# Sixteen half-width products in place of four full ones, in one aggregation of a stack of graph layers in fp32

## The chip, the cores and the metric

The kernel runs on one core of one Trainium2 chip. The metric is the device time of one execution in microseconds (us). In this text TensorE (PE in the profile) does the matmuls, ScalarE (ACT) the activations, VectorE (DVE) the elementwise work.

## The reference, cut to what matters

32 graphs of 512 nodes with 128 features pass four layers, each with its own normalisation and residual. The change touches one line of the last layer, the product of the adjacency matrix with the messages:

```
def _L3_gnn_ref(h, A, W_msg, b_msg, W_ih, b_ih, W_hh, b_hh):
    ...
    msg_pre = jnp.einsum('bnh,kh->bnk', h, W_msg) + b_msg
    m = jnp.tanh(jnp.einsum('bnm,bmh->bnh', A, msg_pre))      # <- this product
    gi = jnp.einsum('bnh,kh->bnk', m, W_ih) + b_ih
    ...
```

## The kernel before

The kernel does not issue its instructions where they are written. Each is recorded with an engine, a duration, what it reads and what it writes. A planner, a small simulation with a priority queue for each engine, then interleaves the 32 graphs and issues everything in the order that this simulation found. The framework below it still moves some instructions.

```
def t_mm(n):
    return n * 0.00167 + 0.008            # us planned for a matmul of n columns

# ... cut ...
def mm(ps, out_of, lhs, rhs, n, start, stop, reads, part=None):
    op("PE", t_mm(n), lambda: nc.tensor.matmul(out_of(ps.ap()), lhs(), rhs(), start=start, stop=stop),
       reads, [(ps, part) if part is not None else ps])

# ... cut ...
def aggregate(ps, feats, lo, m, start=True, stop=True):
    for c in range(NC):                   # NC = 4 blocks of 128 nodes
        mm(ps, lambda t: t, lambda c=c: feats.ap()[:, c, lo:lo + D], lambda c=c: m.ap()[:, c, :], N,
           start and c == 0, stop and c == NC - 1, [(feats, {c}), (m, {c})])
# ... layers 0 to 2 left out ...
psa = plan.bank("agg")
aT2 = buf("s8", (P, NC, N), "aT2")
# ... aT2 is loaded ...
aggregate(psa, msg, 0, aT2)               # D = 128 output rows, N = 512 columns, 4 matmuls
mT = buf("s2", name="mT")
op("ACT", t_act(N), lambda: nc.scalar.activation(mT.ap(), psa.ap(), AF.Tanh), [psa], [mT])
```

Elsewhere each normalisation ends on ScalarE, which writes a tile `h` in four pieces, and TensorE then transposes each piece into `ps_t`.

Of the kernel before, what the change touches and what calls it, by code (L numbers as in the profile page):

```python
# [19 lines left out]
B, N, D = 32, 512, 128  # L20
NC = N // P
# [186 lines left out]
def gnn_stack(  # L208
# [33 lines left out]
    def t_mm(n):  # L242
        return n * 0.00167 + 0.008
# [10 lines left out]
    def op(*args, **kwargs):  # L254
        return plan.op(*args, **kwargs)
# [10 lines left out]
# [3 lines that stand above are left out]
# [58 lines left out]
    def program(b):  # L327
        plan.batch = b

        def buf(tag, shape=(P, N), name=None):  # L330
            return plan.buf(tag, shape, name)
# [57 lines left out]
        def aggregate(ps, feats, lo, m, start=True, stop=True):  # L389

            for c in range(NC):
                mm(ps, lambda t: t, lambda c=c: feats.ap()[:, c, lo:lo + D], lambda c=c: m.ap()[:, c, :], N,
                   start and c == 0, stop and c == NC - 1, [(feats, {c}), (m, {c})])
# [163 lines left out]
        msg = buf("s2", rows_shape, "msg")  # L557
        tt(msg, lambda: nc.vector.tensor_add(msg.ap(), psm.ap().rearrange("p (c v) -> p c v", c=NC), along(r_sb, R_L3_MSG, D, NC)),  # L558
           N, [psm, RS])
        psa = plan.bank("agg")  # L560
        aT2 = buf("s8", (P, NC, N), "aT2")
        op("SP", 0.1, lambda: nc.sync.dma_start(aT2.ap(), adjt[b].rearrange("(c p) n -> p c n", p=P)), [], [aT2], land=5.3)
        aggregate(psa, msg, 0, aT2)
        mT = buf("s2", name="mT")
        op("ACT", t_act(N), lambda: nc.scalar.activation(mT.ap(), psa.ap(), AF.Tanh), [psa], [mT])

# [27 lines left out]
    for b in range(B):  # L594
        program(b)
# [41 lines left out]
```

## Time and profile before

| | before |
|---|---|
| time | 2489.16 us median of 2 runs (2486.97 to 2491.35) |
| TensorE busy | 2419.9 of 2485.6 us |
| next engine, VectorE, busy | 1136.9 us |
| the product that changes | 128 matmuls, 256 records |

The prediction below shows how this is read. Columns: who waited for whom, total us, number of waits, longest us.

```profile
PE ps_agg L267 <- DVE sd L418: 9.9, 22, 0.6
PE ps_t L383 <- ACT h L375: 8.8, 3, 4.1
```

TensorE hardly ever stands still for another engine: 8.8 us for the transposes of `h`, in three waits.

### The profile page before, as it was taken

The page shows a single profiled execution, that of the slowest core. Times are in us where ns is not written, and L with a number is a line of the kernel's source. Part 1 is how long each engine was busy: PE and PEld are TensorE (multiplying, and loading weights), DVE is VectorE, ACT ScalarE, POOL GpSimd, SP SyncE. Part 2 cuts the span into 40 slices and gives each one's busy share as a digit, 9 for nine tenths or more (in the row PEclk, how much of TensorE's full clock was granted, in tenths as well). Part 3 has the DMA queues.
Part 4 walks back from the last instruction along what each step waited for, and adds up shares of the span by engine and source line. Part 5 has one row for each costly group of instructions (what it writes and reads, how often), then busy time and mean ns, then how long its engine had stood idle before and what let it go on. Part 6 is the DMA issues. An engine that isn't in the chain of part 4 may idle for free. (4 is left out here: it accounts for less than half of the span.)

```text
span 2485.6 us, 23454 instructions
## 1 busy us (share of the span) xinstructions
PE 2419.9 (97%) x8898; PEld 1466.4 (59%) x8898; DVE 1136.9 (46%) x2832; ACT 744.0 (30%) x1633; POOL 253.7 (10%) x199
## 2 busy tenths in 40 slices
PE   5899999999999999999999999999999999999997
PEld 4556566556566556566565665565665666655654
DVE  5334455444454444454444554444544444544343
ACT  3221333332333322333322333223333223333121
POOL 1110111100011101011101111010111010110000
PEclk8999999999999999999999999999999999999998
DMA  8011111111112111122111121111111121211000
GB/s 245 20 51 51 64 35 64 66 58 51 51 51 64 60 51 64 35 68 64 60 51 64 34 64 60 55 59 51 51 64 59 51 64 35 68 51 64 13 5 9
DMA packets 123489, 139.67 MB, mean 56 GB/s; under 512 B 36592, under 2 KB 69360, under 8 KB 123376
## 3 DMA queue, kind: packets, MB, share of 16 engines
q1 hardware_dynamic: 122368, 134.36, 16.9%
q10 hardware_dynamic: 1008, 3.81, 0.4%
q8 instruction: 70, 1.15, 0.2%
q14 instruction: 43, 0.35, 0.1%
HBM read 129.64 MB, written 8.52 MB: 56 GB/s over the span
## 5 line engine op out<-in xcount | busy, mean ns | idle before, releaser
L267 PE MATMUL ps_agg<-aT,sd 128*128 128x512 f32 x1024 | 504.5, 595 | 10.5 <-DVE sd L418 9.9
L267 PEld LDWEIGHTS ps_sd<-w_sb,f 128*128 128x128 f32 x1792 | 335.0, 190 | 252.9 <-issue 186.3
L267 PE MATMUL ps_sd<-w_sb,f 128*128 128x256 f32 x1792 | 482.0, 381 | 0.8 <-ACT f L541 0.8
L267 PE MATMUL ps_agg<-a,sd 128*128 128x512 f32 x1024 | 479.0, 592 | 0.0
L363 POOL TENSOR_TENSOR sc<-v,neg_half 128x4 f32<-128x4 f32 (+1 forms) x128 | 150.0, 1172 | 1933.7 <-DVE v L430 1046.8
L541 ACT ACTIVATE f<-ps_agg,cf_sb 128x512 f32<-128x512 f32 x128 | 88.0, 687 | 768.6 <-PE ps_agg L267 767.1
L418 DVE TENSOR_TENSOR sd<-ps_sd,rf_sb 128x512 f32<-128x512 f32 x256 | 175.9, 687 | 309.7 <-PE ps_sd L267 309.7
L267 PEld LDWEIGHTS ps_agg<-a,sd 128*128 128x128 f32 x1024 | 187.4, 190 | 195.8 <-issue 194.2
L375 ACT ACTIVATE h<-xr,nb,sc 128x128 f32<-128x128 f32 x384 | 158.1, 482 | 366.8 <-DVE nb L371 366.8
L267 PEld LDWEIGHTS ps_agg<-aT,sd 128*128 128x128 f32 x1024 | 189.4, 190 | 129.9 <-issue 92.8
L267 PE MATMUL ps_agg<-f,w_sb 128*128 128x512 f32 x448 | 228.7, 593 | 0.0
L429 DVE TENSOR_REDUCE stat<-a 128x4 f32<-128x2048 f32 x32 | 73.1, 2286 | 312.1 <-DMA a<-in_adj 312.1
L267 PE MATMUL ps_agg<-aT,rep 128*128 128x512 f32 x256 | 134.9, 609 | 4.2 <-DVE rep L481 4.2
L267 PE MATMUL ps_agg<-a,rep 128*128 128x512 f32 x256 | 132.0, 597 | 0.0
L267 PE MATMUL ps_agg<-aT,msg 128*128 128x512 f32 x256 | 124.0, 595 | 1.1 <-DVE msg L558 1.1
L525 DVE TENSOR_TENSOR a<-a,rows 128x512 f32<-128x512 f32 x128 | 116.5, 911 | 5.0 <-PE ps_agg L267 3.3
L575 DVE TENSOR_TENSOR g<-ps_gate,r_sb 128x512 f32<-128x512 f32 x128 | 79.5, 683 | 78.4 <-PE ps_gate L267 78.4
L267 PEld LDWEIGHTS ps_gate<-w_sb,hT 128*128 128x128 f32 x512 | 89.6, 193 | 36.0 <-issue 29.7
L267 PE MATMUL ps_gate<-w_sb,hT 128*128 128x256 f32 (+1 forms) x512 | 104.6, 329 | 0.0
L418 DVE TENSOR_TENSOR sd<-ps_sd,r_sb 128x512 f32<-128x512 f32 x64 | 44.2, 691 | 131.4 <-PE ps_sd L267 131.4
L456 DVE SCALAR_TENSOR_TENSOR z<-ps_lin,sc,r_sb 128x128 f32<-128x128 f32 x128 | 36.2, 343 | 143.4 <-PE ps_lin L267 143.3
L267 PE MATMUL ps_agg<-aT,h 128*128 128x256 f32 (+2 forms) x384 | 100.8, 384 | 0.0
(90 smaller groups left out, 2657.5 us busy)
## 6 DMA issues: line engine op xcount, KB each, us to landing
aT<-in_adjt SPq DMA_DIRECT2D x64, 1024.0 KB, 5.4
a<-in_adj SPq DMA_DIRECT2D x32, 1024.0 KB, 5.4
rows<-bounce SPq DMA_DIRECT2D x32, 512.0 KB, 4.4
x<-in_x SPq DMA_DIRECT2D x32, 256.0 KB, 2.8
out<-xo SPq DMA_DIRECT2D x32, 256.0 KB, 2.3
raw<-in_raw ACTq DMA_DIRECT2D x2, 768.0 KB, 9.6
w_sb<-in_w ACTq DMA_DIRECT2D x2, 448.0 KB, 6.8
r_sb<-in_brow ACTq DMA_DIRECT2D x1, 704.0 KB, 6.0
```

What stands on the lines that cost most here:

```text
L267: op("PE", t_mm(n), lambda: nc.tensor.matmul(out_of(ps.ap()), lhs(), rhs(), start=start, stop=stop), reads, [(ps, part) if part is not Non ...
L363: op("POOL", 0.35 + 0.17 * n, lambda: nc.gpsimd.tensor_tensor(inv.ap()[:, :n], v8.ap()[:, :n], neg_half[:, :n], op=ALU.pow), [v8, NH], [(i ...
L375: op("ACT", t_act(D, 2), lambda c=c: nc.scalar.activation(h.ap()[:, c, :], xin.ap()[:, c, :], AF.Relu, bias=nb.ap()[:, c:c + 1], scale=inv ...
L418: op("DVE", t_tt(N), lambda ps=ps, h=h: nc.vector.tensor_add(sd.ap()[:, 2 * h:2 * h + 2, :], ps.ap().rearrange("p (j v) -> p j v", j=2), a ...
L429: op("DVE", 2.2, lambda: nc.vector.tensor_reduce(stat.ap(), a.ap(), AX.X, ALU.add), [a], [stat])
L456: op("DVE", 0.28, lambda c=c: nc.vector.scalar_tensor_tensor(z.ap()[:, c * D:(c + 1) * D], ps0.ap()[:, c * D:(c + 1) * D], inv0.ap()[:, NC ...
L525: op("DVE", t_tt(N), lambda m=m, c=c, s=s: nc.vector.tensor_mul(m.ap()[:, c, :], m.ap()[:, c, :], rows.ap()[:, s, :]), [(m, {c}), rows], [ ...
L541: op("ACT", t_act(N, 1), lambda ps=ps, i=i, f_new=f_new: nc.scalar.activation(f_new.ap(), ps.ap(), AF.Tanh, bias=cf_sb[:, i:i + 1]), [ps, ...
L575: op("DVE", t_tt(N), lambda ps=ps, c=c: nc.vector.tensor_add(g.ap()[:, c, :], ps.ap(), r_sb[:, R_L3_G:R_L3_G + 4 * D]), [ps, RS], [(g, {c})])
```

## The change

A matmul with 64 columns of weights fills one half of the array, and two such matmuls with different halves can run side by side. The change splits each full product (128 output rows, 512 columns) into four: left or right half of the rows, first or second half of the columns, in the order left, right, left, right. Done in perfect pairs, that would be the same work in the same time.

```
-        aggregate(psa, msg, 0, aT2)
+
+        for c in range(NC):
+            for v, i in ((0, 0), (1, 1), (0, 1), (1, 0)):
+                mm(psa, lambda t, v=v, i=i: t[v * D // 2:(v + 1) * D // 2, i * N // 2:(i + 1) * N // 2],
+                   lambda c=c, v=v: msg.ap()[:, c, v * D // 2:(v + 1) * D // 2],
+                   lambda c=c, i=i: aT2.ap()[:, c, i * N // 2:(i + 1) * N // 2], N // 2,
+                   c == 0 and v == i, c == NC - 1 and v != i, [(msg, {c}), (aT2, {c})])
```

Each half product goes through `mm` and so is planned at `t_mm(256)` = 0.44 us, one after the other: 7.0 us for a graph instead of 3.5.

## The prediction

> **What bounds the kernel now.** I read the first page, then a table of three stretches (edges against middle), then the groups of matmuls with their waits, then one undisturbed pass of the layer-3 aggregation in the timeline and the chain of waits.
>
> ```profile
> span 2485.6 us, 23454 instructions
> PE 2419.9 (97%) x8898; PEld 1466.4 (59%) x8898; DVE 1136.9 (46%) x2832; ACT 744.0 (30%) x1633; POOL 253.7 (10%) x199
> ```
>
> TensorE (PE) is busy 97% of the span and the next engine 46%. A busy share can deceive, so I ask where the 66 us without a matmul lie. Columns of the next view: stretch, length, busy us of each engine, granted TensorE clock, DMA share, GB/s.
>
> ```profile
> core 0: us, PE busy (x) PEld busy (x) DVE busy (x) ACT busy (x) POOL busy (x), PEclk, DMA share, GB/s
> 0.00:100.00 100.00, 68.72 (x254) 46.30 (x255) 52.10 (x160) 37.84 (x92) 18.43 (x19) 0.88 0.54 159
> 100.00:2400.00 2300.00, 2282.23 (x8406) 1378.16 (x8405) 1061.24 (x2621) 693.23 (x1518) 233.28 (x178) 1.00 0.17 54
> 2400.00:2485.60 85.60, 68.94 (x242) 41.92 (x240) 23.57 (x51) 12.88 (x23) 2.02 (x2) 0.91 0.02 7
> ```
>
> 31 us of the idle time are in the first 100 us (loading) and 17 us in the last 86 us. In the 2300 us between, only 18 us are idle, under 1%. The 32 graphs overlap so well that nothing waits there but for TensorE. Every microsecond added to its stream is added to the end; there is no slack to hide it in.
>
> Now the piece that changes. First the groups that touch the message tile (duration in ns: min/median/max), then the last graph's aggregation in the timeline (start, length), and its step in the chain of waits.
>
> ```profile
> L267 PEld LDWEIGHTS ps_agg<-aT,msg x256: 186/192/249, 174.1 to 2469.8; 128*128 128x128 f32 x128
> L267 PE MATMUL ps_agg<-aT,msg x256: 592/592/697, 174.2 to 2470.3; 128*128 128x512 f32 x128
> ```
>
> ```profile
> 2467.27 3.60 PE L267 MATMUL ps_agg<-aT,msg 128*128 128x512 f32 x8
> 2467.70 0.19 PEld L267 LDWEIGHTS ps_agg<-aT,msg 128*128 128x128 f32 x1 [0.24 <-issue]
> 2468.13 0.19 PEld L267 LDWEIGHTS ps_agg<-aT,msg 128*128 128x128 f32 x1 [0.24 <-issue]
> 2468.56 0.19 PEld L267 LDWEIGHTS ps_agg<-aT,msg 128*128 128x128 f32 x1 [0.24 <-issue]
> ```
>
> ```profile
> 2467.43 3.43 PE ps_agg L267 x8
> ```
>
> Three readings. (a) The kernel issues 4 matmuls per graph, 128 in all, and the trace has 256 records: each fp32 matmul leaves two records, each with its own weight load. (b) A record lasts 592 ns, but eight take 3.43 us, so one follows the other every 0.429 us: 512 columns at 0.84 ns. The other 592 - 427 = 165 ns is the way through the array, hidden under the next record. (c) A weight load of 0.19 us starts while the matmul before it runs and is hidden too. Where it was not hidden (the maximum, 697 ns) the record is 697 - 592 = 105 ns longer; that is what 128 columns of weights cost in the open.
>
> **What the Trainium skill says.** "FP8 and Floating Point Precision", TensorE Precision Notes: true FP32 takes four passes through the array. The trace agrees: two records a matmul, each at 0.84 ns a column, twice the 1/2.4 ns of one pass at the 2.4 GHz that "TensorE: Matmul & The Clock Gate" gives in its opening table. The same page, Part 3, The mechanism, has matmuls in different parts of the array run at the same time while they start and end strictly in program order; the trace has no such matmul, all its weights are 128*128. "TensorEngine Tiling (Array Packing)", Key Properties, says that changing the tiling mode, as opposed to the tile, drains TensorE. No run here shows it yet; the trace has one mode only. The same page's Overview recommends tiling where a dimension is 64 or less. Here all are 128 or more: the full array is already filled, so even perfect packing can only equal the time before.
>
> **The change part by part.** Removed: 128 matmuls of 512 columns, 256 records x 0.429 = 109.8 us. Added: 16 x 32 = 512 matmuls of 64 output rows x 256 columns, 1024 records. A 256-column record follows its neighbour every 0.216 us (the chain of waits has eight ps_gate records in 1.73 us). Weight bytes loaded double, in loads of 64 columns that stay hidden. DMA, DVE, ACT and POOL work is the same; the semaphores are the same but for a few more waits of TensorE on itself for buffers.
>
> The arithmetic in the array is unchanged only if a left half and a right half run side by side all the time. The diff lists left, right, left, right, so the neighbours suit; but the kernel's own scheduler deals the instructions out singly. I built both kernels and read the order of instructions on TensorE. The 512 half matmuls stand in 311 runs, with full-array matmuls of other graphs between: 204 runs of one, 59 of two, 15 of three, 31 of four, one of five and one of sixteen.
>
> Step 1, streaming. In a run of L half matmuls there are 2L records, in order, L1 L1 R1 R1 L2 L2 and so on. The two records of one matmul use the same half and cannot overlap; the second of one and the first of the next can. So a run takes (L + 1) x 0.216 us, and all take (512 + 311) x 0.216 = 177.8 us. Against 109.8 us that is +68 us. A single half matmul, 204 of them, leaves the other half of the array idle for its whole 0.43 us.
>
> Step 2, the change of mode. Each run has a change in and a change out, 622 in all. If a change drains the array, the tail of 0.165 us is in the open, and then the weights: 0.105 us for 128 columns on the way out, half of it, 0.053, on the way in (an estimate by columns). In: 0.218; out: 0.270; 311 x 0.488 = +152 us.
>
> Sum of steps 1 and 2: +220 us, so 2489 + 220 = 2709 us. All of it lies on TensorE and so on the path that sets the end.
>
> **The rivals.**
> *The mode change is free, halves overlap*: +68 us, 2557 us. For it: hundreds of transposes sit among the matmuls and TensorE shows no gap. Against it: the skill's sentence, and transposes use the whole array.
> *Free change, but fp32 halves do not overlap*: 1024 x 0.216 - 109.8 = +111 us, 2600 us. For it: no fp32 pair has been seen side by side in this trace. Against it: the skill's packed matmuls run together.
> *No overlap and full drain*: +111 + 152 = +263 us, 2752 us.
> *A dearer drain* of some 0.4 us a change with overlap: 68 + 622 x 0.4 = +317 us, 2806 us. Nothing in the profile measures it.
> *No loss at all*, because pairs fill the array: that needs runs of even length and free changes. Even if a pair overlapped wholly, 204 singles x 0.432 = 88 us, plus 59 twos x 0.432, 15 threes and 31 fours x 0.864, a five and the sixteen, 156 us together, is still 46 us more than 109.8, just under 2%. This is the best case that the order allows.
>
> **Range and chances.** I give overlap with drain about 40%, overlap or none with free changes 15% each, no overlap with drain 20%, something dearer 10%. Their weighted mean is 0.4 x 2709 + 0.15 x 2557 + 0.15 x 2600 + 0.2 x 2752 + 0.1 x 2806 = 2688; I say 2690. The range is 2550 to 2785, from the free case to a little over drain without overlap. Slower by over 2% means above 2539 us: 0.93. Within 2% needs the best case or cheaper: 0.06. Faster: 0.01, since nothing is removed from the engine that sets the end.
>
> **What would show it.** Step 1: two records of different halves, in one of the runs of four or sixteen, start within a few ns of each other or at least 0.2 us apart in a ladder, and the last graph's run of sixteen takes near 17 x 0.216 = 3.7 us rather than 32 x 0.216 = 6.9. Step 2: at each change, the first record after it starts some 0.2 to 0.3 us later than its predecessor's columns would allow, and its weight load no longer starts under the matmul before. Sign of being wrong: the middle of the trace shows a TensorE that waits for another engine, or weight loads of the halves that start under full matmuls with the usual spacing.

## The result, and the profile after

The changed kernel took 2681.53 us, median of 2 runs (2679.68 to 2683.38), against 2489.16. The ratio is 1.0778, with a 95% interval of 1.0752 to 1.0804. Here and below a ratio is the mean time of one kernel's fast runs over that of the other's of the same rounds, so it is not quite the ratio of the medians.

The page's head and the middle stretch of the table by stretches, of the changed kernel:

```profile
span 2681.6 us, 25052 instructions
PE 2566.8 (96%) x9666; PEld 1477.3 (55%) x9666; DVE 1129.8 (42%) x2832; ACT 754.3 (28%) x1633; POOL 253.5 (9%) x199
```

```profile
100.00:2590.00 2490.00, 2425.22 (x9130) 1390.11 (x9129) 1052.58 (x2619) 703.78 (x1518) 233.10 (x178) 1.00 0.16 49
```

There are 768 more matmul records, as many as the change adds (1024 less 256). The clock is the same. TensorE is still "96% busy", so the busy row alone hides most of what happened. In the middle its visible idle time grew from 18 to 2490.00 - 2425.22 = 65 us.

The groups of the message tile (min/median/max ns), and a single half product in the middle of the run with a full-array product on either side:

```profile
L267 PEld LDWEIGHTS ps_agg<-aT,msg x1024: 132/136/231, 173.6 to 2666.1; 128*64 128x64 f32 x171
L267 PE MATMUL ps_agg<-aT,msg x1024: 378/379/689, 173.6 to 2666.3; 128*64 128x256 f32 x171
```

```profile
1199.10 1.45 PE L267 MATMUL ps_agg<-aT,sd 128*128 128x512 f32 x3
1199.54 0.19 PEld L267 LDWEIGHTS ps_agg<-aT,sd 128*128 128x128 f32 x1 [0.24 <-issue]
1200.48 0.19 PEld L267 LDWEIGHTS ps_agg<-aT,msg 128*64 128x64 f32 x2 [0.76 <-issue]
1200.48 0.65 PE L267 MATMUL ps_agg<-aT,msg 128*64 128x256 f32 x2
1201.06 0.30 PEld L267 LDWEIGHTS ps_sd<-w_sb,f 128*128 128x128 f32 x2 [0.39 <-issue]
1201.06 0.70 PE L267 MATMUL ps_sd<-w_sb,f 128*128 128x256 f32 x2
```

The reader should look at the weight loads. In the prediction's timeline of the kernel before, each load starts under the matmul ahead of it, after 0.24 us. Here the load of the half product waits 0.76 us and starts in the same instant as its own matmul, and the same happens on the way out at 1201.06. The load is no longer hidden, and it starts only after the columns ahead have gone through. The three full records before it start 0.43 us apart, so the last starts at 1199.96 and its columns are through at 1200.39. The half product starts at 1200.48.

From the start, duration and column count of every matmul record I added up where TensorE's time goes. A column takes 0.833 ns, by the shortest records of 592 ns for 512 columns and 272 ns for 128: (592 - 272) / 384. A record outlasts its columns by 0.165 us, and this tail is taken off each end, which the profiler models. What no column covers is a gap. At the 299 changes into the second mode (the array as two halves of 64 columns) in the middle of the run the first columns follow the last ones after 0.147 us (median): 0.096 until the load starts and 0.051 for it. At the 299 changes out it is 0.200 us: 0.096 and 0.104. The sums over the whole kernel, from the first matmul's columns to the last one's:

| us | before | after | difference |
|---|---|---|---|
| columns through the array | 2327.3 | 2375.9 | +48.6 |
| gaps at changes of mode | 0 | 119.7 | +119.7 |
| gaps between full-array products | 135.5 | 163.3 | +27.8 |
| sum | 2462.8 | 2658.9 | +196.1 |

Some of the 119.7 are not the change itself. At 15 changes out, next to a transpose, the gap is 1.1 us on average and 16.8 us in all. The others, at 0.147 and 0.200 us, make some 103 us. The rest, 120 - 103 + 28 = 45 us, I put down to waits for other engines. The list of waits has two lines that grew, by 51 us together:

```profile
PE ps_t L383 <- ACT h L375: 50.5, 48, 5.2
PE ps_agg L267 <- DVE sd L418: 19.1, 30, 1.1
```

TensorE now waits 48 times, 50.5 us in all, for ScalarE's `h` before a transpose. Before, it did so three times, for 8.8 us. The prediction has no such term. One of these waits:

```profile
1080.15 0.38 PE L267 MATMUL ps_agg<-aT,msg 128*64 128x256 f32 x1
...
1080.86 1.65 ACT L375 ACTIVATE h<-xr,nb,sc 128x128 f32<-128x128 f32 x4 [0.62 <-DVE nb L371]
...
1081.41 0.33 PE L383 MATMUL ps_t<-ident,h 128*128 128x128 f32 x1 [0.88 <-ACT h L375]
```

The last record of a run of three half products starts at 1080.15. The transpose, next in order, can only start at 1081.41, when the first piece of `h` is there. The plan counted 3 x 0.44 = 1.31 us for these three; they took 0.86.

### The profile page after: what moved, and what is told of

The parts are those of the page before. It is cut to its first block, busy times and chain, and to the rows that moved or that the text cites. A ratio compares the mean times of both kernels' runs of the same rounds, so it can differ in the third digit from the quotient of the medians.

```text
span 2681.6 us, 25052 instructions
## 1 busy us (share of the span) xinstructions
PE 2566.8 (96%) x9666; PEld 1477.3 (55%) x9666; DVE 1129.8 (42%) x2832; ACT 754.3 (28%) x1633; POOL 253.5 (9%) x199
## 5 line engine op out<-in xcount | busy, mean ns | idle before, releaser
L267 PE MATMUL ps_sd<-w_sb,f 128*128 128x256 f32 x1792 | 503.6, 393 | 1.3 <-ACT f L541 1.3
L267 PEld LDWEIGHTS ps_sd<-w_sb,f 128*128 128x128 f32 x1792 | 315.9, 189 | 237.9 <-issue 191.1
L267 PE MATMUL ps_agg<-aT,msg 128*64 128x256 f32 x1024 | 225.6, 401 | 0.0
L267 PEld LDWEIGHTS ps_agg<-aT,msg 128*64 128x64 f32 x1024 | 75.9, 135 | 136.9 <-issue 115.4
L383 PE MATMUL ps_t<-ident,h 128*128 128x128 f32 x384 | 89.3, 293 | 52.1 <-ACT h L375 50.5
L383 PEld LDWEIGHTS ps_t<-ident,h 128*128 128x128 f32 x384 | 50.4, 142 | 129.7 <-ACT h L375 115.3
L586 ACT ACTIVATE g<-g 128x512 f32<-128x512 f32 x64 | 40.3, 630 | 284.6 <-DVE g L581 284.6
L525 DVE TENSOR_TENSOR a<-a,rows 128x512 f32<-128x512 f32 x128 | 102.1, 798 | 13.0 <-PE ps_agg L267 10.1
```

The lines of the kernel that those rows point to most:

```text
L383: op("PE", 0.11, lambda c=c: nc.tensor.transpose(ps.ap()[:, c * P:(c + 1) * P], h.ap()[:, c, :], ident), [(h, {c}), ID], [(ps, {c})])
L525: op("DVE", t_tt(N), lambda m=m, c=c, s=s: nc.vector.tensor_mul(m.ap()[:, c, :], m.ap()[:, c, :], rows.ap()[:, s, :]), [(m, {c}), rows], [ ...
L586: op("ACT", t_act(N), lambda s=s: nc.scalar.activation(g.ap()[:, s, :2 * D], g.ap()[:, s, :2 * D], AF.Tanh, scale=0.5), [(g, part)], [(g, ...
```

## The experiments

The theory after the result has three parts. (1) Two halves run fully side by side, but a run with an odd number of halves leaves half the array idle. (2) Each run costs 0.147 + 0.200 = 0.35 us for the two changes of mode. (3) The planner, told 0.44 us for each half, builds an order in which TensorE comes to the transposes too early. The rivals: the halves do not overlap, or stream more slowly as such; the new order alone makes the loss; or the changes alone do. All kernels gave correct results. They ran on three other chips than the pair above, each beside the kernel before: e1, e2, e3 and e6 where it takes 2495.07 us, e4, e5 and e7 where it takes 2494.83, e8 and e9 where it takes 2493.27. The only trace of the kernel before, the one in the table above, has a span of 2485.6 us, so a sum of gaps compared with it carries some 6 to 10 us that are not the edit's.

### e1_block_halves and e2_block_full: no interleaving at all

The sixteen halves of a graph become one unit for the planner; in the control, so do the four full products.

```
+        def block():
+            for c in range(NC):
+                for v, i in ((0, 0), (1, 1), (0, 1), (1, 0)):
+                    half(c, v, i)        # the matmul of the change     (e2: full(c), 512 columns)
+        op("PE", NC * t_mm(N), block, [msg, aT2], [psa])
```

> All sixteen half products of a graph in one block: 32 runs of sixteen, so 64 mode changes instead of 622 and no single halves. Theory (halves overlap fully, each change in and out together costs 0.35 us): 32 x 0.35 = 11 us over the block of four full products run beside it, so near 2500 us if the block itself costs nothing. Rival (halves stream slower as such, the loss belongs to the half products): it stays near 2680 us. Rival (no overlap): 110 us more than the block of full products, 2600 us.

> Control of the block: the four full-width products of a graph issued as one block, no column halves. Every theory of the halves expects the time before, 2489 us, plus or minus what the coarser order costs, which this run measures (guess: within 15 us).

Measured: 2523.71 us for the halves (ratio to before 1.0115, interval 1.0100 to 1.0131) and 2512.33 us for the full products (1.0067, 1.0054 to 1.0080). The coarse block itself costs 17 us. Against this control the halves lose 11.4 us (by the intervals, some 5 either way), the 32 x 0.35 = 11 that part 2 of the theory expected. One block of each kernel in the timeline, e1 and then e2:

```profile
1246.42 3.67 PE L565 MATMUL ps_agg<-aT,msg 128*64 128x256 f32 x32
```

```profile
1244.53 3.70 PE L565 MATMUL ps_agg<-aT,msg 128*128 128x512 f32 x8
```

Sixteen half products, 32 records, take as long as four full ones. The halves overlap without a loss, in fp32 too. Both rivals on overlap fall, and my own ladder of (L + 1) steps falls with them: the records of a left and a right product start in pairs, 2 to 8 ns apart. The length alone would mislead, as a ladder of 17 x 0.216 us is 3.67 too; but the 3.67 here holds the tail of 0.165 us and a weight load of 0.05, which leaves 16 steps, not 17.

### e7_left_then_right: how far the overlap reaches

The block of e1 with the order of the halves changed, and the start and stop flags that go with it:

```
-                for v, i in ((0, 0), (1, 1), (0, 1), (1, 0)):    # inside "for c"
+            for v in range(2):                                   # all left ones, then all right ones
+                for c in range(NC):
+                    for i in range(2):
```

> The block of sixteen with all eight left halves issued first, then all eight right ones. If each half of the array works off its own queue however far apart the instructions are, the time equals the block with alternating halves, near 2500 us. If TensorE looks only one or a few instructions ahead, the two halves run one after the other: 32 x 3.45 = 110 us more, 2610 us.

Measured: 2595.91 us (1.0408, 1.0392 to 1.0423), 72 us above e1. A block now takes 6.3 us:

```profile
1280.19 6.31 PE L565 MATMUL ps_agg<-aT,msg 128*64 128x256 f32 x32
```

Of 32 records in this block, as in each of the other 31 blocks, the first twelve follow each other every 0.216 us, alone. Beside the 13th, 6 ns later, the first record of the right half starts, although three left records stand ahead of it in the program. From there to the end of the left ones two run side by side, then the right ones are alone again. The trace does not name the half of a record; this reading takes it that two records of one half never overlap, as none of the first twelve do. So TensorE does look ahead across halves, by about four records here, and no further. The alternating order of the change is needed.

### e3_in_place: the order of before, halves in it

Each full product is replaced on the spot by its four halves, planned at the full product's duration.

```
+        for c in range(NC):
+            op("PE", t_mm(N), lambda c=c: four(c), [(msg, {c}), (aT2, {c})], [psa])   # four(c): the halves of block c
```

> The kernel before with each full product replaced on the spot by its four halves, planned at the full product's duration: the planned order stays, 93 runs of four, eight or sixteen. Theory: streaming +0, 93 x 0.35 = +32 us, no new waits: 2521 us. Rival (new waits of TensorE on ScalarE, not the changes of mode, make the loss): about 2489 us. Rival (no overlap): 2600 us or more.

Measured: 2506.10 us (1.0045, 1.0032 to 1.0057), 11 us above before, not 32. The gaps at its 186 changes do sum to 31.3 us. But the gaps between full-array products fell from 135.5 to 123.3 us, and the fall may be larger against before on this chip. This run is not a clean control: the plan is the same, but in the trace the full-array products stand in another order than before at 28 places (a pair of `ps_gate` products moved by some 45 records). The next pair has no such difference and gives a reading.

### e4_pairs and e9_two_pieces: the changes of mode by themselves

In e4 a left and a right half are always one unit, planned at 0.44 us. In e9 the pair is one full-array product of 256 columns with the same planned duration. TensorE's order of instructions is the same in both, line for line, in the traces too.

```
 e4:    op("PE", t_mm(N // 2), lambda c=c, i=i: pair(c, i), ...)       # left half x columns i, right half x columns 1 - i
 e9:    op("PE", t_mm(2 * P), lambda c=c, i=i: nc.tensor.matmul(       # all rows x 256 columns
            psa.ap()[:, i * 2 * P:(i + 1) * 2 * P], msg.ap()[:, c, :], aT2.ap()[:, c, i * 2 * P:(i + 1) * 2 * P], ...)
```

> A left and a right half always issued together, planned at the 0.44 us that the pair takes: 154 runs, all of even length, 308 changes of mode. Theory: streaming +0, 154 x 0.35 = +54 us, no new waits: 2543 us. Rival (the singles' idle halves and the waits are the whole loss): 2489 us.

> Control for the pairs: each pair of halves replaced by one full-array product of 256 columns, planned at the same duration; TensorE's order of instructions is the same line for line, without a second mode. Theory: the pairs' run minus 308 changes at 0.35 us for in and out, part of which lay over waits that are there anyway: 2522.6 - 54 = 2469 us if none of it was hidden, 2495 us (the time before) if half was. Rival (changes of mode cost nothing here, the pairs lose by their order): 2520 us.

Measured: e4 2522.60 us (1.0119, 1.0102 to 1.0136), e9 2491.35 us (0.9990, 0.9976 to 1.0003). With the same order and no idle halves the 308 changes cost 31 us, by the difference of the times as by that of the two profiled spans (2520.1 - 2489.5); relative to before on each one's own chip it is 30 to 32. The bare gaps would be 154 x 0.347 = 53 us. The sums of gaps show what became of the others: in e4 the changes have 60.5 us, and the gaps elsewhere are 107.8 us against 139.5 in e9. A change that falls in front of a wait only takes the place of part of that wait. So the cost of a change in the open is 0.35 us for in and out, and about 0.2 us of it reached the end in this order. The rival, that changes are free, falls; so does my sentence that TensorE has no slack to hide anything in.

The busy row would not have shown any of this. The same 2290 us of e4, then of e9:

```profile
100.00:2390.00 2290.00, 2266.50 (x8951) 1368.08 (x8950) 1040.21 (x2569) 690.41 (x1496) 230.64 (x176) 1.00 0.22 54
```

```profile
100.00:2390.00 2290.00, 2266.43 (x8612) 1410.80 (x8611) 1052.71 (x2612) 697.87 (x1516) 243.14 (x178) 1.00 0.21 54
```

TensorE is equally "busy" in both, as a record counts as busy for 0.165 us after its columns, and the gaps at a change lie mostly under that tail.

### e6_full_quarters and e8_quarters_true: the planned duration by itself

e6 keeps the sixteen pieces and the planned 0.44 us of the changed kernel, but each piece is a full-array product of 128 columns that takes 0.22 us. Its order on TensorE is close to that of the changed kernel, not the same: in the traces 112 of the 8642 other records stand elsewhere. e8 differs from e6 in one number.

```
 e6:  op("PE", t_mm(N // 2), lambda c=c, i=i: nc.tensor.matmul(        # planned 0.44 us
 e8:  op("PE", t_mm(P), lambda c=c, i=i: nc.tensor.matmul(             # planned 0.22 us
          psa.ap()[:, i * P:(i + 1) * P], msg.ap()[:, c, :], aT2.ap()[:, c, i * P:(i + 1) * P], ...)
```

> The changed kernel's fine split and its too long planned duration (sixteen pieces of 0.44 us in a graph) but each piece a full-array product of 128 columns: nearly the changed kernel's order of instructions, no second mode, no idle half. Theory: only the new waits remain, about +40 us (2510 to 2550). Rival (the new order and its waits make most of the loss): 2600 to 2680 us.

> The sixteen full-array quarters, with the one edit that the planner is told their true duration of 0.22 us in place of 0.44. Theory (the extra 86 us of that kernel are waits made by planning with too long a duration): back to 2480 to 2500 us. Rival (the fine split itself, its many short products or weight loads, makes the loss): 2560 us or more.

Measured: e6 2581.20 us (1.0350, 1.0335 to 1.0364), e8 2495.35 us (1.0006, 0.9993 to 1.0018). A wrong number for the planner, without a half product or a second mode anywhere, costs 86 us. That is more than the 40 I expected, and less than the rival's figure, but it shows that part of the change's loss can come about with no use of the halves at all. The waits of e6 and of e8:

```profile
PE ps_t L383 <- ACT h L375: 85.5, 76, 5.2
```

```profile
PE ps_t L383 <- ACT h L375: 23.7, 30, 4.1
```

It is the same wait as in the changed kernel, and it goes with the wrong duration: it makes 62 of the 86 us by which e6 and e8 differ. The list is not a loss by itself, though: e9 has 18.1 us of this wait where before has 8.8, and takes the same time.

### e5_true_plan: the changed kernel with one number corrected

```
-   mm(psa, ..., N // 2, ...)                       # planned t_mm(N // 2), 0.44 us
+   op("PE", t_mm(N // 2) / 2, ...)                 # the same matmul, planned 0.22 us
```

> The changed kernel with one edit: the planner is told half the duration for a half product, as two run side by side. The built order has 215 runs, of which 91 are single halves. Theory: streaming 317 slots of 0.432 us against 110 us, +27; changes 215 x 0.35 = +75; waits as before: 2591 us. If the extra waits of the changed kernel (about 40 us, ScalarE's h ahead of the transposes) do not come from the wrong duration, they stay and it takes about 2630 us.

Measured: 2565.93 us (1.0290, 1.0274 to 1.0305), 71 us above before where the changed kernel is 192 above. The wait for `h` is back to where e4 and e8 have it:

```profile
PE ps_t L383 <- ACT h L375: 16.6, 27, 4.1
```

The number corrected, the planner also leaves fewer and longer runs: 215 for 311, and 91 single halves for 204. The columns take 2354.9 us, 27.6 more than before, as computed. The changes have 79.9 us of gaps, and 29 us of other gaps vanished (135.5 to 106.2, against before's only trace). I had expected 102 us and forgot again that changes take the place of waits. Most of the loss of the changed kernel, 121 of 192 us, thus went with a planned duration that is twice too long. It did not all go as waits: of the 118 us between the two profiled spans, 57 are gaps between full-array products, 40 gaps at changes and 21 idle halves. The last two need both the halves and the order that the wrong number made.

No version beats the kernel before. The best two, e9 (0.9976 to 1.0003) and e8, cannot be told from it, and neither has halves.

## Why the prediction was right or wrong

The time was 2681.53 us, 8 us under the predicted 2690 and inside the range of 2550 to 2785. "Slower by over 2%", at 0.93, was right. That nearness is luck. 2690 was the weighted mean of five cases, the favoured one stood at 2709, and in its sum errors of both signs met.

- **What bounds the kernel.** Right: TensorE sets the end, and the other engines do the same work as before. "There is no slack to hide it in" was wrong. I read slack from the busy row, which showed 18 us idle in the middle. From column to column the gaps of the kernel before sum to 135.5 us; e9 against e4 shows some of them taking up 22 of 53 us of changes.
- **Step 1, streaming, +68.** Measured +48.6. The step that failed is "2L records, in order": the halves do not form a ladder. A left and a right record start within 2 to 8 ns, and a run of L takes one slot of 0.43 us for each pair or single. This is what the prediction computed as its best case for the order, 156 us or +46, and set aside; its own terms add up to 158, +48.
- **Step 2, the change of mode, +152.** The mechanism was right, and its term was mis-sized: 0.347 us a run, not 0.488, some 103 us. The part for the weights was right (0.104 and 0.051 measured, 0.105 and 0.053 predicted). The wait ahead of it was taken as 0.165 us, the whole tail of a record; it is 0.096.
- **What was missing, +45.** The prediction counts the order of instructions only for its runs. It did not ask what the planner believed about the new instructions. The page's list of waits shows 50.5 us for `h`, and e5, e6 and e8 show that this wait comes with the planned duration. The prediction had named "a TensorE that waits for another engine" as a sign of being wrong, and in this part it was.
- **The rivals.** Free changes and halves that do not overlap were both rejected by e4 with e9 and by e1 with e2. The dearer drain of 0.4 us a change did not come.

So 48.6 + 103 + 45 = 197 (the profiled spans differ by 196, the medians by 192) stood against 68 + 152 = 220. What stays open: why the wait ahead of the load is 0.096 us; how the gaps at changes and the waits mesh in the changed kernel itself, since no full-array kernel has exactly its order; and why TensorE looks ahead just as far as e7 shows.

## What to carry to other kernels

Splitting a product that already fills the array gained nothing here in any version, and every stretch of half products inside full-array work cost a change in and out of the mode, up to 0.35 us, so keep them in long even runs or leave them out. Where a planner orders the program, a new instruction needs its true duration: here correcting that number took back 121 us, and all that the halves still cost with it corrected was 71. Judge TensorE by the spacing of its columns, not by its busy row.

## What the Trainium skill lacked or had wrong

- "TensorEngine Tiling (Array Packing)", Key Properties, says that a change of tiling mode drains TensorE and gives no figure. Here the columns pause 0.147 us on the way into the 64-column mode and 0.200 us on the way out, of which 0.051 and 0.104 us are the weight load in the open.
- "TensorE: Matmul & The Clock Gate", Part 3, The mechanism, says that matmuls start and end strictly in program order. In e7, as read above, the first right-half record starts 6 ns after the 13th left-half record, ahead of three left-half records, two of them the whole eighth left product, that precede it in the program. The small offset between tiles that the same part gives under Measured speedup vs the span model (about 4 ns) agrees with the 2 to 8 ns here.
- No page says whether fp32 matmuls, which leave two records each here, overlap in two column halves. They do: 32 half records in 3.67 us, 8 full ones in 3.70 us.
